# Splitting the last half-norm of a decoder layer: seven blocks first, the eighth added late

## The chip, the cores and the metric

The kernel runs on one core of one Trainium2 chip. The metric is the device time of one execution in microseconds (us); the median of the runs is compared. Times inside a profile are counted from the start of its span, the stretch from the first to the last instruction.

## The reference

One decoder layer on x of shape (8, 100, 1024), float32, with a norm behind each of three parts:

```
x = layernorm(x + attn(x))
x = layernorm(x + xattn(x, ctx))
x = layernorm(x + ffn(x))                # the part concerned here

layernorm(x) = (x - mean(x)) / sqrt(mean((x - mean(x))^2) + 1e-5)      # over the 1024 features
ffn(x)       = (silu(x @ w_gate.T) * (x @ w_up.T)) @ w_down.T          # 1024 -> 4096 -> 1024
```

## The kernel before

Activations lie with features on the partitions: the 1024 features are KT = 8 blocks of P = 128 rows, and the 800 tokens are two halves of N = 400 columns. A "block" below is a tile slice of 128 x 400 floats, and `y` of one half holds eight of them, the residual stream on which the norm works. A matmul in full float32 shows up in the profile as a pair of TensorE instructions; the projections instead use a split of weights and activations in a high and a low part of type fp32r, with three single matmuls for each product (lines 86 to 88 of `mm3`).

The mean and the variance of a token are sums over partitions and blocks. They are made by a matmul with a constant 128x128 matrix, which adds over the partitions and leaves the result on all of them: `onem` holds 1/1024, `onem7` holds 1/896 for the mean of seven blocks alone. The matmul's input is a sum over blocks, formed on VectorE.

The tail of the program (from line 965) works off the last quarter of the down projection. For each half, and for each m from 0 to 7, the weight block is loaded and split (`load_raw`, `w_split`), `proj` multiplies (24 matmuls into a PSUM bank), line 972 adds the bank to `y[:, m]`, and `add_up` (line 253) adds the block to the running sum `s1`. When all eight are done, `norm_root` takes the norm: the mean from `s1` (line 278), eight subtractions (line 280), squares on ScalarE (line 259), the variance (line 284), a copy out of PSUM (line 286), and `inv_root`: Ln, Exp and Square on ScalarE (lines 113, 116, 118) and two VectorE operations (lines 119, 120), one Newton step on the inverse root. `scaled` then multiplies the eight blocks by the result (line 270), and behind each block SyncE's queue issues the store of 200 KB to the output (line 273).

For half 0, `norm_root` adds the eight squared blocks on VectorE (line 264) and sends one pair of matmuls to TensorE. For half 1 it is called with `idle_pe=True`: each squared block goes to TensorE as it is, eight pairs accumulating in one PSUM bank, and no sum is made on VectorE.

The norms behind the two attention parts (`out_proj`) already take half 1 in another way, with two functions that the tail does not use before the change:

```
def norm_early(y, s1, p):                                                     # lines 292 to 300
    n = y.shape[2]
    mean = bank("s")[:, :n]
    nc.tensor.matmul(mean, onem7, s1, start=True, stop=True)
    for m in range(KT - 1):
        nc.vector.tensor_tensor(y[:, m], y[:, m], mean, ALU.subtract)
    var = bank("v")[:, :n]
    nc.tensor.matmul(var, onem, squares(y, p, range(KT - 1)), start=True, stop=False)
    return mean, var
```

`norm_late` (lines 302 to 313) ends what `norm_early` began. The eighth block comes in relative to the mean of the other seven; the mean of that block (times 1/1024) is `delta`, the amount by which the true mean differs from the mean of seven. The variance is the sum of all squares less `delta` squared (lines 306, 308, 309), and every block is reduced by `delta` (line 312) before it is scaled.

`squares` uses two buffers for the squared blocks and two for the running sum, so the square after next has to wait until the sum has taken one in. PSUM has three banks of tag "a", four of "s" and one of "v"; the projections take "a" and "s" in turn.

The order of instructions on each engine isn't written by hand. The framework's planner lists them at build time from the program's order as priority and from its own estimates of when operands are ready; on the chip each engine then runs its list in order and waits where it must. What the estimates get wrong becomes waiting.

Of the kernel before, what the change touches and what calls it, by code (L numbers as in the profile page):

```python
# [11 lines left out]
ALU = mybir.AluOpType  # L12
# [7 lines left out]
N = NB * T  # L20
KT = D // P
# [18 lines left out]
def decoder_layer(ctx, tc, xT, cT, w1, wo1, w2, wo2, wc, w3, wd, gw, qw, kw, trig, dec, mask, out):  # L40
    nc = tc.nc

    def sbuf(name, bufs, side=None):
        return tc.tile_pool(name=name, bufs=bufs, side=side, reuse_waits="tile")
# [8 lines left out]
    def bank(tag):  # L53
        return ps.tile([P, 512], F32, tag=tag, name=tag, bufs=banks[tag])
# [7 lines left out]
    def split(dst, src):  # L62

        split2(dst[:, 0], dst[:, 1], src)
# [25 lines left out]
    def mmw(acc, w, k, rh, rl, start, stop):  # L90
        c = slice(k * P, (k + 1) * P)
        mm3(acc, w[:, 0, c], w[:, 1, c], rh, rl, start, stop)
# [3 lines left out]
    def acc_tag():  # L96
        turn[0] += 1
        return "as"[turn[0] % 2]

    def proj(w, z, n=N, tag="a"):  # L100
        acc = bank(tag)[:, :n]
        for k in range(KT):
            t = z[k // QT]
            mmw(acc, w, k, t[:, 0, k % QT, :n], t[:, 1, k % QT, :n], k == 0, k == KT - 1)
        return acc
# [4 lines left out]
    def inv_root(pool, ss, eps, n=N, pin=False):  # L110

        r = pool.tile([P, n], F32, tag="r0", name="r0")
        ln = nc.scalar.activation(r, ss, AF.Ln, bias=eps)
        if pin:
            tc.keep_in_program_order(ln)
        nc.scalar.activation(r, r, AF.Exp, scale=-0.5)
        q = pool.tile([P, n], F32, tag="r1", name="r1")
        nc.scalar.activation(q, r, AF.Square)  # L118
        nc.vector.scalar_tensor_tensor(q, ss, eps, q, ALU.add, ALU.mult)  # L119
        nc.vector.scalar_tensor_tensor(q, q, 3.0, r, ALU.subtract, ALU.mult)  # L120
        return q
# [49 lines left out]
    onem = cp.tile([P, P], F32, name="onem")  # L171
# [44 lines left out]
    def out_proj(half, w, load_o, res, yp, ybufs, p, make_z, dst, after=None):  # L216
# [26 lines left out]
        if half == 0:  # L243
            scaled(y, norm_root(y, s1, p), lambda m: dst[half, :, m], z)
        else:
            norm_late(y, early, p, lambda m: dst[half, :, m], z)
# [4 lines left out]
    def add_up(s1, y, m):  # L251
        if m > 0:
            nc.vector.tensor_tensor(s1, y[:, 0] if m == 1 else s1, y[:, m], ALU.add)

    def squares(y, p, ms):
        s2 = None
        for m in ms:
            sq = p.tile([P, y.shape[2]], F32, tag="sq", name="sq", bufs=2)
            nc.scalar.activation(sq, y[:, m], AF.Square)
            if s2 is None:  # L260
                s2 = sq
            else:
                s3 = p.tile([P, y.shape[2]], F32, tag="s2", name="s2", bufs=2)
                nc.vector.tensor_tensor(s3, s2, sq, ALU.add)
                s2 = s3
        return s2

    def scaled(y, r, dst, z=None):
        for m in range(KT):
            nc.vector.scalar_tensor_tensor(y[:, m], y[:, m], -0.5, r, ALU.mult, ALU.mult)  # L270
            if z is not None:
                split(z[m // QT][:, :, m % QT], y[:, m])
            nc.sync.dma_start(out=dst(m), in_=y[:, m])

    def norm_root(y, s1, p, idle_pe=False):
        n = y.shape[2]
        mean = bank("s")[:, :n]
        nc.tensor.matmul(mean, onem, s1, start=True, stop=True)
        for m in range(KT):
            nc.vector.tensor_tensor(y[:, m], y[:, m], mean, ALU.subtract)  # L280
        var = bank("v")[:, :n]
        for m in range(KT) if idle_pe else [KT]:
            ms = [m] if idle_pe else range(KT)
            nc.tensor.matmul(var, onem, squares(y, p, ms), start=m == 0 or not idle_pe, stop=m >= KT - 1)
        vs = p.tile([P, n], F32, tag="vs", name="vs")
        nc.scalar.copy(vs, var)
        return inv_root(p, vs, eps_ln, n)
# [4 lines left out]
    def norm_early(y, s1, p):  # L292
# [6 lines that stand above are left out]
        nc.tensor.matmul(var, onem, squares(y, p, range(KT - 1)), start=True, stop=False)  # L299
        return mean, var  # L300

    def norm_late(y, early, p, dst, z):
        n = y.shape[2]
        delta = bank("s")[:, :n]
        nc.tensor.matmul(delta, onem, y[:, KT - 1], start=True, stop=True)
        nc.tensor.matmul(early[1], onem, squares(y, p, [KT - 1]), start=False, stop=True)
        vs = p.tile([P, n], F32, tag="vs", name="vs")
        nc.scalar.activation(vs, delta, AF.Square)
        nc.vector.tensor_tensor(vs, early[1], vs, ALU.subtract)
        r = inv_root(p, vs, eps_ln, n)  # L310
        for m in range(KT):
            nc.vector.tensor_tensor(y[:, m], y[:, m], delta, ALU.subtract)
        scaled(y, r, dst, z)
# [9 lines left out]
    def load_raw(src):  # L323
        st = wp.tile([P, KT * P], F32, tag="wst", name="wst", bufs=3)
        if isinstance(src, list):
            for i, s in enumerate(src):
                nc.sync.dma_start(out=st[:, i * H:(i + 1) * H].rearrange("p (u c) -> p u c", u=QT), in_=s)
        else:
            nc.sync.dma_start(out=st, in_=src)
        return st  # L330

    def w_split(src):
        w = wp.tile([P, 2, KT * P], FR, tag="w", name="w", bufs=4)
        split(w, src)
        return w
# [281 lines left out]
    early = []  # L617
    with sbuf("l2", 2) as p:
        for kv in range(NKV):
            for i0, i1 in ((0, 4), (4, 6)) if kv == 0 else ((0, 2), (2, 4), (4, 6)):  # L620
# [8 lines left out]
                for half in range(2):  # L629
                    bs = slice(half * NB, (half + 1) * NB)  # L630
                    for i in range(i0, i1):
# [12 lines left out]
                        r = inv_root(p, ss, eps_k)  # L644
# [10 lines left out]
    with sbuf("cx", 2) as p, sbuf("c1", 1) as p1:  # L655
        for b in range(B):
            if b > 0:
                load_context(b)
            for kv in range(NKV):
# [86 lines left out]
                r = p.tile([P, N], F32, bufs=1, tag="r0", name="r0")  # L746
# [183 lines left out]
    def down_w(q, m):  # L930


        w = wd[q * QT:(q + 1) * QT, m // QT].rearrange("u p c -> p u c")
        c = m % QT * 2 * P
        return [w[:, :, c + i * P:c + (i + 1) * P] for i in range(2)]
# [30 lines left out]
    with sbuf("ln3", 2, "right") as lnp:  # L966
        for half in range(2):
            y = rows(half)
            s1 = lnp.tile([P, N], F32, tag="s1", name="s1", bufs=2)
            for m in range(KT):  # L970
                acc = proj(w_split(load_raw(down_w(QT - 1, m))), z3[half], tag=acc_tag())
                nc.vector.tensor_tensor(y[:, m], y[:, m], acc, ALU.add)
                add_up(s1, y, m)
            r = norm_root(y, s1, lnp, idle_pe=half == 1)
            scaled(y, r, lambda m, half=half: out[:, m, half * N:(half + 1) * N])


# [69 lines left out]
```

## Time and profile before

| | |
|---|---|
| median of 3 runs | 2528.96 us (2527.68 to 2529.01) |
| the profiled execution | 2527.58 us |
| its span | 2525.8 us |
| TensorE busy | 2478.2 us (98%) |
| VectorE busy | 2000.6 us (79%) |
| ScalarE busy | 1353.7 us (54%) |
| last projection matmul ends | 2504.75 us into the span |
| first block of half 1 is scaled (line 270) | at 2518.14 us |

Around TensorE's 98% it should be kept in mind that a share is a mean over the program. From 2504.75 us on there are no projections left, and the 21.05 us to the end of the span are a chain through all engines, in which TensorE is busy for 7.25 us, VectorE for 10.27 us and ScalarE for 6.43 us. The whole change lies in and shortly ahead of that stretch.

### The profile page before, as it was taken

Reading aid. Unit: us, or ns where it says so; the run is one execution under the profiler, and the core shown is the slowest. Engines: PE = TensorE matmul, PEld = TensorE weight load, DVE = VectorE, ACT = ScalarE, POOL = GpSimd, SP = SyncE. Lnnn points to the kernel's source line nnn. Section 1 sums busy time; section 2 is a strip of 40 time slices with the busy share of each in tenths; the row PEclk is TensorE's granted clock in tenths of the full one; section 3 lists DMA queues with packets and bytes.
Section 4 is the critical chain, followed back from the end, with each engine's and each line's share of the span. In section 5 each row is a group of like instructions: output and inputs, shape, how many; then the busy total and the mean of one; then the engine's idle time right before and its main releaser. Section 6 shows DMA issues by size and latency. Waiting matters only on the chain.

```text
span 2525.8 us, 37215 instructions
## 1 busy us (share of the span) xinstructions
PE 2478.2 (98%) x14042; PEld 2440.9 (97%) x14042; DVE 2000.6 (79%) x3106; ACT 1353.7 (54%) x2272; POOL 466.8 (18%) x230
## 2 busy tenths in 40 slices
PE   8999999999999999999999999999999999999997
PEld 8999999998899999999999999999999999998996
DVE  7778876568989798998998998866988777666756
ACT  6666676336667466655656566533554454432222
POOL 0111111002555243433433434100000000000000
PEclk9999999999999999999999999999999999999999
DMA  7333445774444654455554554575455445388742
GB/s 239 110 110 127 136 146 186 240 268 147 143 147 147 202 174 156 151 170 161 163 165 146 163 190 125 199 259 162 137 183 195 163 158 167 127 298 313 249 135 86
DMA packets 232898, 438.16 MB, mean 173 GB/s; under 512 B 47594, under 2 KB 176490, under 8 KB 220302
## 3 DMA queue, kind: packets, MB, share of 16 engines
q1 hardware_dynamic: 231566, 431.59, 51.3%
q0 software_dynamic: 1152, 4.19, 1.1%
q8 instruction: 110, 1.80, 0.3%
q14 instruction: 70, 0.57, 0.1%
HBM read 326.38 MB, written 109.35 MB: 173 GB/s over the span
## 4 chain that ended last, share of the span: by engine, by line
PE 89%; DVE 6%; issue 2%; DMA 1%; ACT 1%; SPq 0%; DVEq 0%; ACTq 0%
PE a L88 18%; PE a L86 18%; PE a L87 17%; PE s L88 9%; PE s L87 9%; PE s L86 9%; PE v L86 2%; PE v L88 2%; PE v L87 2%; PE s L486 1%; PE s L677 1%; DVE r L120 1%; DVE r L119 1%; PE s L148 1%; DVE d L68 1%
## 5 line engine op out<-in xcount | busy, mean ns | idle before, releaser
L86 PE MATMUL a<-big,w 128*128 128x400 f32 (+2 forms) x1824 | 616.3, 339 | 10.5 <-ACT big L67 7.1
L87 PE MATMUL a<-big,w 128*128 128x400 f32 (+2 forms) x1824 | 615.7, 338 | 0.0
L88 PE MATMUL a<-big,w 128*128 128x400 f32 (+2 forms) x1824 | 614.4, 338 | 0.0
L67 ACT CAST w<-wst 128x1024 fp32r<-128x1024 f32 (+1 forms) x243 | 251.8, 1039 | 431.0 <-PE s L88 152.3
L68 DVE TENSOR_TENSOR w<-wst,w 128x1024 fp32r<-128x1024 f32 (+1 forms) x243 | 297.7, 1227 | 120.2 <-ACT w L67 119.0
L86 PEld LDWEIGHTS a<-big,w 128*128 128x128 f32 x1824 | 343.7, 189 | 12.3 <-ACT big L67 7.4
L87 PEld LDWEIGHTS a<-big,w 128*128 128x128 f32 x1824 | 344.5, 189 | 1.4 <-DVE big L68 0.3
L88 PEld LDWEIGHTS a<-big,w 128*128 128x128 f32 x1824 | 344.2, 189 | 1.0 <-DVE w L68 0.3
L86 PE MATMUL s<-big,w 128*128 128x400 f32 x680 | 236.0, 347 | 0.1
L87 PE MATMUL s<-big,w 128*128 128x400 f32 x680 | 234.7, 345 | 0.0
L88 PE MATMUL s<-big,w 128*128 128x400 f32 x680 | 234.6, 346 | 0.0
L125 POOL PARTITION_ALL_REDUCE ss<-sq x56 | 159.4, 2851 | 337.4 <-DMA zd<-y 166.9
L600 POOL PARTITION_ALL_REDUCE kss<-ksq x64 | 162.3, 2536 | 138.7 <-ACT ksq L599 136.9
L86 PE MATMUL a<-z,w 128*128 128x400 f32 x504 | 174.5, 346 | 8.2 <-ACT r L118 4.3
L88 PE MATMUL a<-z,w 128*128 128x400 f32 x504 | 174.9, 347 | 0.7 <-DVE w L68 0.7
L87 PE MATMUL a<-z,w 128*128 128x400 f32 x504 | 175.0, 347 | 0.0
L87 PE MATMUL s<-z,w 128*128 128x400 f32 x416 | 144.5, 347 | 2.3 <-DVE z L68 2.3
L86 PE MATMUL s<-z,w 128*128 128x400 f32 x416 | 145.2, 349 | 0.0
L88 PE MATMUL s<-z,w 128*128 128x400 f32 x416 | 145.1, 349 | 0.0
L711 ACT ACTIVATE s<-s,rk 128x400 f32<-128x400 f32 x160 | 88.3, 591 | 97.0 <-DVE sm L733 65.0
L86 PEld LDWEIGHTS s<-big,w 128*128 128x128 f32 x680 | 127.6, 188 | 1.4 <-ACT w L67 0.4
L87 PEld LDWEIGHTS s<-big,w 128*128 128x128 f32 x680 | 127.6, 188 | 1.1
(274 smaller groups left out, 5562.6 us busy)
## 6 DMA issues: line engine op xcount, KB each, us to landing
wst<-in_w SPq DMA_DIRECT2D x135, 512.0 KB
w<-wcd SPq DMA_DIRECT2D x64, 1024.0 KB
wst<-in_wo SPq DMA_DIRECT2D x64, 512.0 KB
wst<-in_wd SPq DMA_DIRECT2D x80, 256.0 KB
hd<-h SPq DMA_DIRECT2D x12, 1400.0 KB
big<-o1d SPq DMA_DIRECT2D x16, 800.0 KB
qd<-d SPq DMA_DIRECT2D x32, 400.0 KB
q<-qd SPq DMA_DIRECT2D x32, 400.0 KB
```

Source lines behind the costliest of these rows:

```text
L67: nc.scalar.copy(hi, src)
L68: nc.vector.tensor_tensor(lo, src, f32(hi), ALU.subtract)
L86: nc.tensor.matmul(acc, lh, rh, start=start, stop=False, skip_group_check=chain)
L87: nc.tensor.matmul(acc, lh, rl, start=False, stop=False, skip_group_check=chain)
L88: nc.tensor.matmul(acc, ll, rh, start=False, stop=stop, skip_group_check=chain)
L119: nc.vector.scalar_tensor_tensor(q, ss, eps, q, ALU.add, ALU.mult)
L120: nc.vector.scalar_tensor_tensor(q, q, 3.0, r, ALU.subtract, ALU.mult)
L125: nc.gpsimd.partition_all_reduce(y, x, P, op)
L148: nc.tensor.transpose(tr[0:T, b * P:(b + 1) * P], vt[:, b * T:(b + 1) * T], ident)
L486: nc.tensor.matmul(bt(o)[:, b], vv[:, b * P:(b + 1) * P], pf[:, b], start=True, stop=True)
L600: nc.gpsimd.partition_all_reduce(ss[:, at], sq[:, at], P, RED.add)
L711: nc.scalar.activation(sc, sp, AF.Copy, scale=rk[:, c:c + 1])
```

## The change

For half 1 of the last norm, the tail takes up the two functions that the other norms use. After block 6 has been added to the sum, `norm_early` takes the mean of seven blocks, subtracts it from them, squares them, adds the squares on VectorE, and opens the variance's accumulation. The mean of seven is subtracted from block 7 as well, before block 7's projection is added to it. After that `norm_late` does the rest. Block 7 is no longer added to `s1`; the eight accumulating pairs of matmuls of line 284 are gone, and with them the argument `idle_pe`. Half 0 is computed as before.

```
-    def norm_root(y, s1, p, idle_pe=False):
+    def norm_root(y, s1, p):
...
         var = bank("v")[:, :n]
-        for m in range(KT) if idle_pe else [KT]:
-            ms = [m] if idle_pe else range(KT)
-            nc.tensor.matmul(var, onem, squares(y, p, ms), start=m == 0 or not idle_pe, stop=m >= KT - 1)
+        nc.tensor.matmul(var, onem, squares(y, p, range(KT)), start=True, stop=True)
...
-    def norm_late(y, early, p, dst, z):
+    def norm_late(y, early, p, dst, z=None):
...
             for m in range(KT):
+                last = half == 1 and m == KT - 1
+                if last:
+                    early = norm_early(y, s1, lnp)
+                    nc.vector.tensor_tensor(y[:, m], y[:, m], early[0], ALU.subtract)
                 acc = proj(w_split(load_raw(down_w(QT - 1, m))), z3[half], tag=acc_tag())
                 nc.vector.tensor_tensor(y[:, m], y[:, m], acc, ALU.add)
-                add_up(s1, y, m)
-            r = norm_root(y, s1, lnp, idle_pe=half == 1)
-            scaled(y, r, lambda m, half=half: out[:, m, half * N:(half + 1) * N])
+                if not last:
+                    add_up(s1, y, m)
+            dst = lambda m, half=half: out[:, m, half * N:(half + 1) * N]
+            if half == 0:
+                scaled(y, norm_root(y, s1, lnp), dst)
+            else:
+                norm_late(y, early, lnp, dst)
```

## The prediction, written before the changed kernel was run

> **What bounds the kernel now.** First the page's busy times: TensorE is at 98% of the span, so over the program only its work counts. But the change touches the end, where a mean says nothing. So I read next the chain of work that ended last, in order of time, from the last projection on (start, duration, both us, engine, tile, line):
>
> ```profile
> 2504.57 0.20 PE a L88
> 2504.79 0.58 DVE y L972
> 2505.39 0.58 DVE s L253
> 2506.02 0.95 PE s L278 x2
> 2507.00 0.58 DVE y L280
> 2507.60 0.55 ACT sq L259
> 2508.19 6.32 PE v L284 x16
> 2514.54 0.50 ACT vs L286
> 2515.06 0.64 ACT r L113
> ...
> 2517.53 0.59 DVE r L120
> 2518.14 0.58 DVE y L270
> ```
>
> Nothing overlaps here: every microsecond from 2504.79 to the end is on the path. From 2504.79 to line 113 at 2515.06 it is 10.27 us, the stretch that the change rewrites; from 2515.06 to the first scaled block 3.08 us; from there to the end of the span 7.66 us (eight scalings at 0.485 apart, the last store). These two stay. The 6.32 us of line 284 are eight rounds of 0.79: subtract, square, matmul pair, with two square buffers.
>
> Second, VectorE's timeline ahead of that, to see when the early half could begin:
>
> ```profile
> 2498.41 3.97 DVE L270 SCALAR_TENSOR_TENSOR y<-y,r 128x400 f32<-128x400 f32 x8
> 2502.30 0.56 DVE L972 TENSOR_TENSOR y<-y,s 128x400 f32<-128x400 f32 x1
> 2502.90 0.57 DVE L253 TENSOR_TENSOR s<-s,y 128x400 f32<-128x400 f32 x1
> 2504.79 0.57 DVE L972 TENSOR_TENSOR y<-y,a 128x400 f32<-128x400 f32 x1 [1.32 <-PE a L88]
> ```
>
> Half 0's scaling holds VectorE until 2502.38, so block 6, whose projection ended about 2500.4, enters the sum only at 2503.47. That is 1.3 us before the last projection ends, not a whole projection (4.37 us).
>
> Third, the same pair of functions at work in the second norm, VectorE and then TensorE:
>
> ```profile
> 1743.82 1.93 DVE L264 TENSOR_TENSOR s<-s,sq 128x400 f32<-128x400 f32 x3
> ...
> 1751.21 3.94 DVE L312 TENSOR_TENSOR y<-y,s 128x400 f32<-128x400 f32 x8 [0.87 <-ACT vs L308]
> 1755.06 0.57 DVE L309 TENSOR_TENSOR vs<-v,vs 128x400 f32<-128x400 f32 x1
> ```
>
> ```profile
> 1749.80 0.83 PE L305 MATMUL s<-y,onem 128*128 128x400 f32 x2
> 1753.21 0.83 PE L299 MATMUL v<-s,onem 128*128 128x400 f32 x2
> 1753.88 0.83 PE L306 MATMUL v<-sq,onem 128*128 128x400 f32 x2
> ```
>
> Running sums of squares come (1.93 - 0.57) / 2 = 0.68 apart, paced by the two buffers. Two float32 pairs take 0.67 + 0.83 = 1.50. And there the planner put all eight late subtractions ahead of line 309. In that norm other projections fill TensorE, so the wait cost little; in the tail nothing is left to fill.
>
> Fourth, the clock. Windows after the last matmul of the program (it ends at 2514.51):
>
> ```profile
> 2516.00:2516.50 0.50, 0.00 (x0) 0.00 (x0) 0.00 (x0) 0.47 (x2) 0.00 (x0) 1.00 0.00 0
> 2517.00:2517.50 0.50, 0.00 (x0) 0.00 (x0) 0.49 (x1) 0.00 (x0) 0.00 (x0) 0.50 0.00 0
> ```
>
> The third number from the right is the granted TensorE clock: it falls to half about 2.4 us after TensorE goes idle. It also falls inside the program, behind a gap of 2.27 us at 605.1: from about 608.9 to 612.0 matmuls start 0.33 apart instead of 0.18.
>
> **What the Trainium skill says.** "TensorE: Matmul & The Clock Gate", What's actually happening: the array runs at half clock after an idle window of about 3.4 us, the window runs freely, and about as long a busy stretch is needed to get full speed back. The trace agrees in kind: 0.5 behind the end, and some 3.3 us at half pace at 609. "VectorE: DVE Perf Modes", the perf-mode tier table: a float32 `tensor_tensor` has no faster mode; here 0.566 each. "Perfetto Trace Analysis", Optimizing Scalar/DVE Operations: part of the profiled latency overlaps with the next instruction; here eight subtractions take 3.94, so 0.482 from start to start.
>
> **The change part by part.** Removed from the path: line 253 for block 7, the mean pair at 2506.02, the first subtraction and square, the eight rounds and the copy, all in the 10.27 us. In their place:
>
> 1. The mean of seven. Ready at 2503.47; in the two earlier norms the pair starts 0.39 after its input, so 2503.9; bounds 2503.50 (at once) and 2504.75 (behind the last projection, if the planner thinks it late, as it does with half 0's mean, placed between two projections). A pair within the stream gives its result after 0.87: subtractions start at 2504.77. The pair pushes the last projection from 2504.75 to 2505.42, free: its reader in VectorE's queue comes only at about 2509.2. Without that cover it would cost 0.67.
> 2. Seven subtractions, the one for block 7, the first sum: nine VectorE operations, 8 x 0.482 + 0.57 = 4.42, to 2509.19. The squares beside them are ScalarE's and fit (0.53 each), but only two buffers exist, so the third waits for the first sum.
> 3. Line 972 for block 7 goes into the wait that follows (0.482; the wait is 0.57). Five more sums: 0.57 until the next square, 4 x 0.68, 0.57: 3.86, to 2513.05. Here VectorE has replaced TensorE as the adder, with 3.3 us more work (seven blocks need six sums of 0.566) on the path.
> 4. `delta`: its pair from about 2509.7, its square on ScalarE, both done before 2512, beside step 3: free.
> 5. The two variance pairs, from 2513.09: 1.50 at full clock, and at half clock 3 x 0.667 + 0.87 = 2.87. TensorE has been idle from 2505.42 to 2509.7 and, but for `delta`, to 2513. That is longer than both gaps above, so I take half clock: 2515.96. Full clock would give 2514.59.
> 6. Line 309 instead of the copy: 0.03 + 0.57 + 0.02, so Ln at 2516.58, against 2515.06.
> 7. Eight late subtractions, 3.86: six fit between 2513.05 and 2515.96, the rest (room for 3.7) while ScalarE does Ln, Exp and Square (1.77). Free, if the planner splits them so. If all eight stand ahead of line 309, as in the second norm, they end at 2517.0, 1.0 late. If one stands between two sums, it costs about 0.3.
> 8. The stores are the same eight, behind the same scalings on SyncE's queue, which is idle in between. No weight load or split is queued behind any wait: the last split was at 2488.08.
>
> Sum: 2516.58 - 2515.06 = +1.5 us. The span becomes 2527.3, the profiled execution 2529.1 (it was 2527.58), and with the same shift the median 2528.96 + 1.5 = 2530.5.
>
> The unknowns and their ends: step 1, -0.4 to +0.85 around my value; step 5, -1.37 to 0; step 7, 0 to +1.0, and up to about +1 for subtractions among the sums. What excludes a great gain is a count. After the mean VectorE has 24 operations (7 + 1 + 6 + 1 + 8 + 1) and lines 119 and 120 before it may scale: 24 x 0.482 + 1.25 = 12.8 us. From 2504.37, the earliest, that is 2517.2, against 2518.14. So without reordering ahead of the mean the gain is at most about 0.95 us.
>
> **The rivals.**
> A. *Hidden as meant.* Mean at once, clock kept up, subtractions well placed: +1.5 - 0.4 - 1.37 = -0.3, at the very best -0.95: 2528.0 to 2529. For it: small matmuls in the old tail kept the clock at 1.0 over gaps of 1.3. Against: the new gap is over 4 us.
> B. *The wait goes to VectorE's list.* All late subtractions ahead of line 309, or the mean behind the last projection: +2.4 to +4, so 2531.4 to 2533. For it: the order in the second norm, and half 0's mean.
> C. *Slower beyond doubt.* The planner puts late subtractions ahead of the remaining sums, since it believes `delta` ready and the squares not. Each costs 0.482 on the path; all eight 3.86, with step 5 +5.4: 2534.3. It decides from (5.06 - 1.5) / 0.482 = 7.4 of them. Against: a sum has the earlier place in the program, so it wins whenever its square is there.
> D. *Another order before the tail.* If the planner took block 6 before half 0's scaling and overlapped the whole early half, the end could come up to 6 us sooner (the late half alone: 0.6 + 0.95 + 0.5 + 0.6 + 3.1 plus the eight subtractions that don't fit): 2523. Against: the count above, since VectorE's work has to be done anyway.
>
> **How the numbers follow.** 0.2% is 5.06 us, about what a measurement of this kernel can tell from no change. Forecast (+0.5 to +2.4) 48%, A 17%, B 24%, C 8%, D 3%. Within 0.2% lie the forecast, A and B: 89%; slower C, 8%; faster D, 3%. The range leaves out C and D and the edges of A and B: 2527.2 to 2533.2, which also holds the 1.3 us by which runs of one kernel differ.
>
> **What would show it.** Right: line 299's pair starts near 2513 and lines 299 and 306 together take nearly 2.9 us, at clock 0.5; from 2504.4 VectorE is almost without gaps; Ln starts about 1.5 us later than before. Step 1 is wrong if the mean's pair starts outside 2503.5 to 2504.8; step 3 if the sums aren't 0.68 apart; step 5 if the pairs take 1.5; step 7 if line 309 waits for VectorE and not for TensorE. The prediction is wrong as a whole if the time before 2495 us changes at all: then the planner has moved more than the tail.

## The result

| | before | changed |
|---|---|---|
| median of 22 runs each | 2527.88 us | 2532.32 us |
| ratio, 95% interval | | 1.0018 (1.0012 to 1.0025) |
| the profiled execution | 2527.58 us | 2534.26 us |
| its span | 2525.8 us | 2532.5 us |
| last projection matmul ends | 2504.75 | 2506.32 |
| half 1's Ln starts (line 113) | 2515.06 | 2521.77 |
| from the one to the other, "the tail" | 10.31 us | 15.45 us |
| from Ln to the end of the span | 10.74 us | 10.73 us |

The change made the kernel slower by 4.4 us (the interval gives 3.0 to 6.3). The two profiled executions differ by 6.7, but 1.6 of that lies ahead of the end of the last projection, where every engine's list of instructions is the same in both kernels; runs of one kernel differ by more than that. What belongs to the change is the tail: 15.45 - 10.31 = 5.14 us.

The chain that ended last, in the changed kernel, cut to the pieces that matter (start, duration, engine, tile, line; line 293 is here the mean's pair, 295 the subtraction of the mean of seven, 310 the late subtraction of `delta`, 297 and 304 the variance's pairs, 307 the variance less `delta` squared; dots stand for pieces left out):

```profile
2506.14 0.18 PE a L88
2506.32 0.69 PE s L293 x2
...
2507.03 3.45 DVE y L295 x7
...
2515.07 2.48 DVE y L310 x5
2517.55 0.50 DVE s L264
...
2518.09 1.70 PE v L297 x2
2519.79 1.35 PE v L304 x2
...
2521.16 0.59 DVE vs L307
...
2521.77 0.64 ACT r L113
```

Before, this stretch was led by TensorE, with 6.32 us of small pairs. Now VectorE leads from 2507.03 to 2518.05, with one square on ScalarE in between, and TensorE comes in only at the end. Three things stand out. The mean's pair stands behind all matmuls of the last projection, so VectorE starts 0.71 us behind the projection's end. Between the fifth and the sixth of the six sums (line 264) there are late subtractions on the path, work that nobody needs yet. And the two pairs of the variance last 3.05 us.

TensorE's timeline of the same stretch shows what it did in the meantime (the brackets give the idle time ahead and what ended it; line 303 is `delta`'s pair, and line 974 adds block 7's projection), and the windows show the granted clock (third number from the right):

```profile
2506.16 0.83 PE L293 MATMUL s<-s,onem 128*128 128x400 f32 x2
2511.99 1.70 PE L303 MATMUL s<-y,onem 128*128 128x400 f32 x2 [4.99 <-DVE y L974]
2518.09 1.70 PE L297 MATMUL v<-s,onem 128*128 128x400 f32 x2 [4.40 <-DVE s L264]
2519.59 1.54 PE L304 MATMUL v<-sq,onem 128*128 128x400 f32 x2
```

```profile
2508.00:2509.00 1.00, 0.00 (x0) 0.00 (x0) 1.00 (x4) 0.65 (x2) 0.00 (x0) 1.00 0.00 0
2509.00:2510.00 1.00, 0.00 (x0) 0.00 (x0) 1.00 (x4) 0.00 (x0) 0.00 (x0) 0.64 0.00 0
2510.00:2511.00 1.00, 0.00 (x0) 0.00 (x0) 1.00 (x4) 0.00 (x0) 0.00 (x0) 0.50 0.00 0
2518.00:2519.00 1.00, 0.91 (x2) 0.58 (x3) 1.00 (x3) 0.00 (x0) 0.00 (x0) 0.50 0.00 0
```

TensorE ends the mean's pair at 2506.99, waits 5 us, does `delta`'s pair, waits 4.4 us. The clock is full at 2508, half from 2510 on, and still half when the variance's pairs come. A pair takes 1.5 to 1.7 us where the mean's took 0.83.

Last, VectorE's timeline where the list goes astray, and ScalarE's squares of blocks 6 and 7:

```profile
2512.06 2.61 DVE L264 TENSOR_TENSOR s<-s,sq 128x400 f32<-128x400 f32 x4
2514.58 2.97 DVE L310 TENSOR_TENSOR y<-y,s 128x400 f32<-128x400 f32 x6
2517.47 0.57 DVE L264 TENSOR_TENSOR s<-s,sq 128x400 f32<-128x400 f32 x1
```

```profile
2514.17 1.07 ACT L259 ACTIVATE sq<-y 128x400 f32<-128x400 f32 x2
```

Six late subtractions stand in a block ahead of the last sum. ScalarE had that sum's square, the first of the two, done about 2514.7, so the sum waited 2.8 us for its place in the list and for nothing else.

### The profile page after: what moved, and what is told of

The parts are those of the page before. It is cut to its first block, busy times and chain, and to the rows that moved or that the text cites. A ratio compares the mean times of both kernels' runs of the same rounds, so it can differ in the third digit from the quotient of the medians.

```text
span 2532.5 us, 37209 instructions
## 1 busy us (share of the span) xinstructions
PE 2477.2 (98%) x14032; PEld 2440.2 (96%) x14032; DVE 2005.0 (79%) x3120; ACT 1352.5 (53%) x2272; POOL 471.0 (19%) x230
## 4 chain that ended last, share of the span: by engine, by line
PE 87%; DVE 7%; DMA 2%; ACT 2%; issue 2%; SPq 0%; DVEq 0%; ACTq 0%
PE a L88 17%; PE a L86 17%; PE a L87 17%; PE s L88 9%; PE s L87 9%; PE s L86 9%; PE v L86 2%; PE v L88 2%; PE v L87 2%; PE s L484 1%; DVE r L120 1%; PE s L675 1%; DVE r L119 1%; DVE w L68 1%; PE s L148 1%
```

## The experiments

The theory after the result, "order and clock": the loss is the six sums that VectorE took over, a list with six subtractions at the wrong place, a TensorE that has gone to half clock by the time it is wanted, and a mean that starts behind the last projection. The main rival, "saturation": VectorE has 24 operations to do ahead of the scaling, so their order doesn't matter, and the clock only fills a time that would pass anyway. The tail is measured as above, in one profile of each kernel.

| kernel | tail, us | median, us | ratio to before |
|---|---|---|---|
| before | 10.31 | 2526.77 | 1 |
| changed | 15.45 | 2532.32 | 1.0018 (1.0012 to 1.0025) |
| sums_alone | 13.58 | 2529.67 | 1.0008 (1.0000 to 1.0017) |
| subs_behind_sums | 12.77 | 2528.93 | 1.0008 (0.9999 to 1.0016) |
| behind_warm | 11.48 | 2527.71 | 1.0002 (0.9993 to 1.0010) |
| early_pe | 9.75 | 2526.44 | 0.9995 (0.9987 to 1.0003) |

The four experiments ran on one chip and are compared with 41 runs of the kernel before, median 2526.77; the changed kernel's row is that of the first table, with its own comparison. Neighbours in the table can't be told apart by their times alone. Their tails can, piece by piece: where two lists agree, so do the profiles, as with the 10.74 and 10.73 us behind Ln above.

**One part alone: VectorE adds the squares, no early half.** On the kernel before:

```
-            r = norm_root(y, s1, lnp, idle_pe=half == 1)
+            r = norm_root(y, s1, lnp, idle_pe=False)
```

> The kernel before, with one part of the change alone: half 1's squares are added on VectorE and go to TensorE as one pair, with no early half. The metric of all these runs is the tail, from the end of the last projection to the start of half 1's Ln (line 113): 10.3 us before, 15.45 us in the changed kernel. Theory (order and clock: the new VectorE sums, a list that puts late subtractions ahead of the last sum, and a TensorE that has gone to half clock): eight subtractions, the first sum, six more 0.68 apart, then one pair at half clock (1.70): tail 13.5, +3.2 us on before. Rival (the clock has no part in it, a pair takes 0.83 or 0.95): +2.4. Rival (VectorE's additions cost no more than TensorE's rounds of 0.79): within 0.5 of before.

The tail was 13.58. TensorE's timeline has the one pair:

```profile
2515.02 1.70 PE L284 MATMUL v<-s,onem 128*128 128x400 f32 x2 [9.09 <-DVE s L264]
```

```profile
2515.00:2516.70 1.70, 1.68 (x2) 0.50 (x2) 0.00 (x0) 0.00 (x0) 0.00 (x0) 0.50 0.00 0
```

It waited 9.09 us and then ran at half clock. So the change of the adder alone, without a misplaced subtraction, costs 3.3 us. About 0.8 of that is the clock, by an estimate from the 1.70 us here and the 0.94 us that the mean's pair took in the same run at full clock; the rest is the sums. Both rivals are out: sums on VectorE aren't as cheap as TensorE's rounds, and 13.58 fits a pair at half clock and not one of 0.83.

**VectorE's list put right.** On the changed kernel, in `norm_late` for the tail alone, where `z` is None (`sums` keeps the additions of line 264; `issue_after` fixes the order of issue and adds no wait):

```
-        nc.vector.tensor_tensor(vs, early[1], vs, ALU.subtract)
+        late = range(KT)
+        if z is None:
+            late = range(4, KT)
+            with tc.issue_after(sums[-1].ins):
+                for m in range(4):
+                    nc.vector.tensor_tensor(y[:, m], y[:, m], delta, ALU.subtract)
+        v = nc.vector.tensor_tensor(vs, early[1], vs, ALU.subtract)
         r = inv_root(p, vs, eps_ln, n)
-        for m in range(KT):
-            nc.vector.tensor_tensor(y[:, m], y[:, m], delta, ALU.subtract)
+        if z is None:
+            with tc.issue_after(v.ins):
+                for m in late:
+                    nc.vector.tensor_tensor(y[:, m], y[:, m], delta, ALU.subtract)
...
```

> The changed kernel, with VectorE's list alone altered: four of the late subtractions stand behind the last sum of squares and four behind line 307, none ahead of the last sum. Theory (order and clock): the last sum ends 9.0 us behind the end of the last projection in place of 11.7, so tail 12.75, 2.7 us shorter than in the changed kernel, total about 1.7 above before. Rival (saturation: VectorE has 24 operations to do before it may scale, and in what order it does them is all one): tail within 0.5 us of 15.45.

VectorE's timeline, the five sums without a break (lines 266, 314 and 315 are 264, 310 and 307 of the changed kernel):

```profile
2508.21 3.29 DVE L266 TENSOR_TENSOR s<-s,sq 128x400 f32<-128x400 f32 x5
2511.42 2.01 DVE L314 TENSOR_TENSOR y<-y,s 128x400 f32<-128x400 f32 x4
2514.63 0.57 DVE L315 TENSOR_TENSOR vs<-v,vs 128x400 f32<-128x400 f32 x1 [1.20 <-PE v L306]
```

The tail fell by 2.68 to 12.77. TensorE's and ScalarE's lists are unchanged, so the order of VectorE's list alone is worth that. Saturation is refuted: VectorE now even idles 1.20 us ahead of line 315, waiting for TensorE.

**The same, with TensorE kept busy.** Eleven pairs on data that nobody uses, into a bank that nobody reads, seven behind the mean's pair (`means[-1]`) and four behind `delta`'s (`d`):

```
+        if z is None:
+            idle = bank("a")[:, :n]
+            for ins, k in ((means[-1], 7), (d, 4)):
+                with tc.issue_after(ins.ins):
+                    for i in range(k):
+                        nc.tensor.matmul(idle, onem, f32(z3[1][0])[:, 0, i % QT], start=True, stop=True)
```

> The same order as in subs_behind_sums, and eleven float32 matmul pairs on data that nobody uses, seven behind the mean's pair and four behind delta's, which only keep TensorE busy. Theory (order and clock): the two variance pairs take 1.5 us in place of 3.05, Ln comes 1.1 to 1.5 us sooner than in subs_behind_sums, tail 11.3 to 11.6; delta comes some 0.3 us later, which the list covers. Rival (the pairs are slow for another reason, such as waiting for weights after a pause, or saturation): tail within 0.4 us of subs_behind_sums, or longer by what the added pairs hold up.

TensorE's timeline, the variance's pairs behind the last of the idle ones, and a window with the clock:

```profile
2511.66 0.89 PE L299 MATMUL v<-s,onem 128*128 128x400 f32 x2
2512.39 0.83 PE L306 MATMUL v<-sq,onem 128*128 128x400 f32 x2
```

```profile
2510.00:2512.00 2.00, 2.00 (x7) 1.04 (x6) 1.79 (x5) 1.30 (x3) 0.00 (x0) 1.00 0.00 0
```

The granted clock stayed at 1.00 (ScalarE's list differs by the place of one square), the two pairs took 1.56 from first start to last end in place of 3.03, and the tail fell by 1.29. It would have been 1.47, but now line 307's counterpart waits for VectorE. So useless work made the tail shorter, and the slow pairs were the clock's doing. The idle pairs also took away the pause ahead of the variance, which the rival blames; but a pause of 1.27 us in the kernel before made a pair only 0.11 us longer (0.94 against 0.83), and in the changed kernel the pair of line 304, right behind another, was slow as well: 0.87 us for each of its two matmuls, against 0.50 here. The times of the two kernels, 2528.93 and 2527.71, agree but don't show it by themselves.

**TensorE adds, as before, in the new order.** In `norm_early` (`pe` is true for the tail), with four late subtractions on each side of line 307:

```
-        nc.tensor.matmul(var, onem, squares(y, p, range(KT - 1)), start=True, stop=False)
+        for ms in [[m] for m in range(KT - 1)] if pe else [range(KT - 1)]:
+            nc.tensor.matmul(var, onem, squares(y, p, ms), start=ms[0] == 0, stop=False)
```

> The changed kernel, with the seven squared blocks of the early half sent to TensorE one by one, as the kernel before does, in place of six sums on VectorE; four late subtractions ahead of line 307 and four behind. Theory: squares and pairs at 0.79 a round from 1.9 us behind the end of the last projection, with delta's pair between them: the variance is complete 8.9 us behind that end and the tail is 9.5, so about 0.8 us below before and 6.0 below the changed kernel. Rival (the early half itself is what costs: its mean, two more rounds of subtractions and VectorE's load): tail over 11, slower than before.

TensorE's timeline, the first five of the seven rounds of the early half:

```profile
2507.01 4.07 PE L298 MATMUL v<-sq,onem 128*128 128x400 f32 x10 [1.23 <-ACT sq L259]
```

The tail was 9.75, 5.7 below the changed kernel and 0.56 below the kernel before, and the granted clock stayed at 1.00. The early half itself isn't a loss: its second round of eight subtractions fits beside TensorE's rounds. The rival, a tail over 11, is refuted. The time, 0.9995 (0.9987 to 1.0003), can't be told from the kernel before.

A second set ran on one chip too and is compared with 57 runs of the kernel before, median 2527.03. Two of its kernels move the end of the last projection itself, so it is counted from the start of that projection to Ln: 14.85 us before and 19.98 changed by the trace's first matmul record of it (the expectations put that start 0.17 later, have 14.68 and 19.82, and so are to be read 0.17 longer here).

| kernel | start of last projection to Ln, us | median, us | ratio to before |
|---|---|---|---|
| before | 14.85 | | 1 |
| changed | 19.98 | | |
| mean_mid | 19.03 | 2531.29 | 1.0015 (1.0009 to 1.0022) |
| early_pe | 14.28 | | |
| early_pe_mid | 13.33 | 2525.72 | 0.9993 (0.9985 to 1.0001) |
| early_mid_sq4 | 12.35 | 2524.48 | 0.9990 (0.9983 to 0.9996) |
| before_sq4 | 14.18 | 2526.58 | 0.9999 (0.9990 to 1.0007) |

**The mean into the last projection.** On the changed kernel, `proj` for block 7 issues its matmuls from k = `held` on (`part`) behind the mean's pair (`means[-1]`):

```
+        part(range(held))
+        if held < KT:
+            with tc.issue_after(means[-1].ins):
+                part(range(held, KT))
...
-                acc = proj(w_split(load_raw(down_w(QT - 1, m))), z3[half], tag=acc_tag())
+                acc = proj(w_split(load_raw(down_w(QT - 1, m))), z3[half], tag=acc_tag(), held=6 if last else KT)
```

> The changed kernel, with TensorE's list alone altered: the pair for the mean of seven stands behind 18 of the 24 matmuls of the last projection in place of behind all of them. Measured here from the start of the last projection to half 1's Ln: 14.68 us before, 19.82 in the changed kernel. Theory (the mean's place is one of the losses, and everything behind it follows from it): the pair starts at once when block 6 has entered the sum, 1.1 us sooner, and so does all that follows: 18.75. Rival (the stretch is bound by what VectorE does later and by the half clock, so an earlier mean only makes a wait longer): within 0.3 of 19.82.

VectorE's timeline of mean_mid, the end of the sum over blocks and the first use of the mean:

```profile
2502.41 0.58 DVE L262 TENSOR_TENSOR s<-s,y 128x400 f32<-128x400 f32 x1
2504.02 3.45 DVE L304 TENSOR_TENSOR y<-y,s 128x400 f32<-128x400 f32 x7 [1.03 <-PE s L302]
```

From the sum's end to the subtractions it is 1.03 us; in the changed kernel it was 1.99. All behind it moved by the same 0.95 us. So the mean's place is one of the losses, of 0.95 us where 1.1 was expected. The time (2531.29) is too coarse to show it.

**early_pe with the mean inside the projection.** The two edits above together.

> early_pe with the mean's pair behind 18 of the last projection's 24 matmuls. early_pe took 14.12 us from the start of the last projection to Ln. Theory: 1.1 less, 13.05, 1.6 us below the kernel before, time 2526.77 - 1.6, about 2525.2. Rival (the last projection, put off by 0.67, now ends last): 13.7 or more.

13.33: again 0.95 less than without the move, where the theory had 1.1, and well below the 13.7 of the rival.

**A version that beats both.** early_pe_mid, with `held=4`, four buffers for squares (`bufs=2` becomes `bufs=4` in `squares`, for the tail), and the pairs of blocks 5 and 6 issued behind `delta`'s pair.

> early_pe_mid with four buffers for squared blocks in the tail in place of two, the mean behind 12 of the 24 matmuls, and the squared blocks 5 and 6 behind delta's pair. The planner then also changes the order of half 0's norm, and block 6 enters the sum sooner. Theory: TensorE becomes the bound, with 24 matmuls and ten pairs at 0.67 without a gap: 11.9 us from the start of the last projection to Ln, 2.8 below the kernel before, about 2524.0. Rival (squares on ScalarE or VectorE's subtractions set the pace even with four buffers): 12.7 or more.

The chain that ended last:

```profile
2504.68 3.36 PE v L309 x10
2508.04 0.69 PE s L315 x2
...
2511.30 0.48 DVE vs L328
```

TensorE runs from the projection through the squares at 0.67 a pair, as the theory said. But the end is 0.3 us later than it said, since line 328 (307 of the changed kernel) waits for four late subtractions, and these waited for ScalarE (the last section); so VectorE's subtractions, which the rival named, do set the last bit of the pace. The run changes the mean's place, the buffers and the order of pairs at once, and with them the planner's order of half 0's norm; what each is worth was not separated. At 0.9990 (0.9983 to 0.9996) it is 2.5 us faster than the kernel before; against the changed kernel's 1.0018 the intervals lie well apart.

**Two more buffers for the kernel before.** Only `bufs=4` for the tail's squares.

> The kernel before with four buffers for squared blocks in the tail in place of two, nothing else in its text. Theory: the rounds of 0.79 are paced by the two buffers, and with four a round is TensorE's own 0.67: eight rounds save 0.9 us, 13.8 from the start of the last projection to Ln. Rival (the rounds are paced by the squares themselves): unchanged, 14.7.

TensorE's eight rounds took 5.64 us in place of 6.31: the two buffers did pace the rounds, for 0.67 us in all, less than the 0.9 expected, since only six of the seven distances between rounds shrank, by 0.11 each. Here too the planner ordered half 0's norm otherwise, ahead of the stretch that is measured. The time (0.9999) doesn't show the gain.

## Why the prediction was right and wrong

The call held: the difference is 0.18% where 0.2% was the bound, and 2532.32 lies in the range. Both held by luck in part. The interval reaches past the bound, and the tail alone grew by 5.14 us, where the bound is 5.06. The range was laid around the median of three runs of the kernel before, 2528.96; over 22 runs it is 2527.88, and from 2528.96 the measured +4.4 would have ended at 2533.4, above the range. The forecast itself, +0.5 to +2.4 around +1.5, did not hold: its centre was 3 us short. And 0.2% is more than has to be granted to chance here: with 22 runs each, the interval of 1.0012 to 1.0025 is clear of 1. By its steps:

1. *The mean of seven*: taken in the middle of its bounds, right behind its input. It stood behind the whole last projection, and the subtractions began 0.71 after that projection's end in place of 0.02: +0.69. The late bound, +0.85, was nearly the right value (the pair starts 0.16 before the projection's last matmul ends); mean_mid shows what the place costs.
2. *Seven subtractions, block 7's, the first sum*: 4.42 predicted, 4.43 measured (2507.03 to 2511.46).
3. *Five more sums*: 3.86 predicted; with an unbroken list 3.89 (subs_behind_sums). In the changed kernel 6.58.
4. *`delta` beside the sums*: free, as predicted.
5. *The variance at half clock*: the half clock came as predicted; 2.87 was the price and 3.05 was measured, +0.18, nearly all of it because the first matmul behind the pause takes 0.83 to the next in place of 0.667. behind_warm gave the full-clock price: 1.56, where 1.50 had been worked out.
6. *Line 307*: as predicted.
7. *Eight late subtractions*: this step failed. It called them "Free, if the planner splits them so", took that for the likeliest, and priced the misplaced ones only as "up to about +1 for subtractions among the sums". Six stood in a block ahead of the last sum: +2.72. The other two stood between that sum and line 307 and were free: they ended at 2519.00, and the variance at 2521.14.

The terms add up: 0.69 + 2.72 + 0.18 beyond the predicted 1.52 are 5.11, against the measured 5.14. (One figure of step 3 is off, but isn't used in the sum: six sums of 0.566 are 3.4 us and not 3.3.) What had been set apart as rival C, late subtractions ahead of sums at 0.482 each, happened for six of eight, at 2.72 / 6 = 0.45 each. Its point of decision, 7.4 of them, wasn't reached. What B had named was in the list too, the mean behind the last projection and all eight late subtractions ahead of line 307; but apart from the mean it was the place ahead of the last sum that cost, and not the place ahead of line 307. The tail's 5.14 us lies past B's +2.4 to +4 (so does the 4.4 of the times, though its interval begins at 3.0), for C's reason added to the late mean. Rival D's new order ahead of the tail did not come about. C's argument against itself, that a sum wins its place whenever its square is there, was made with times of the chip; the list was made beforehand with the planner's own estimates, and on the chip the square was there 2.8 us before the sum's turn. Why the planner thought otherwise wasn't tried.

The signs that were named need care. Step 7's was line 307 waiting for VectorE; it waited for TensorE, 2.16 us, as it should have, and so this sign missed the step that failed. Step 3's caught it: four sums were 0.68 apart, but the last came 3.38 behind the one ahead of it. The time before 2495 did change, by some 1.6 us, without the planner having moved anything there: the lists are the same, and in subs_behind_sums, with the same lists again, the last projection ends at 2502.47.

Rival A, the hidden early half, was not to be had by the change as written: with the list put right and the clock kept (behind_warm, 11.48) and mean_mid's 0.95 us taken off, an estimate of 10.5 is left, and the kernel before has 10.31. The two were not run together. A's bound of 0.95 held under the premise that VectorE makes the sums. early_pe and early_mid_sq4 leave that premise, and only then does the early half gain, early_pe by its tail alone.

## What to carry to other kernels

When work is taken off an engine that idles and given to one that is on the path, price the other engine's loss of clock too: here the sums and the half clock cost 3.3 us before anything was out of place. In a list made at build time, look for operations with no deadline that are ready early, since the planner may put them ahead of work that is on the path, as it did here; fixing their order was worth 2.7 us without one instruction saved. And starting early pays only for the engine whose work shrinks at the end: the same early half was a loss with VectorE as the adder and a gain with TensorE, of 0.6 us, or 1.5 with the mean moved, by the profiles (the times of these two, 0.9995 and 0.9993, don't show it by themselves).

## What the runs showed that had not been expected

Idle matmuls shortened a tail: eleven useless pairs kept the clock at 1.00 and brought Ln 1.29 us forward. At half clock a float32 pair on 128x400 took 1.70 us behind a pause; at full clock it took 0.94 behind a pause and 0.83 in a stream. The mean clock of 0.64 between 2509 and 2510 puts the fall in the changed kernel at about 2509.3, by estimate 2.3 us after TensorE's last matmul; gaps of 1.27 and 1.23 us in the kernel before left it at 1.00.

The late subtractions don't start when `delta` is ready, but when ScalarE has also read it. VectorE's timeline of early_mid_sq4:

```profile
2509.29 2.01 DVE L327 TENSOR_TENSOR y<-y,s 128x400 f32<-128x400 f32 x4 [2.15 <-ACT vs L322]
```

`delta`'s pair ended at 2508.73, ScalarE squared it from 2508.75 to 2509.25, and VectorE began at 2509.29: two readers of one PSUM bank, one after the other, 0.55 us. early_pe and early_pe_mid show the same wait. In the changed kernel it is hidden behind the sums. Whether the hardware or the framework's ordering asks for it was not tried.
